# A decoder layer in fp32: keys and values made a batch ahead and kept in HBM, and the experts' second product in seven half-size products

## The chip, the cores and the metric

The kernel runs on one core of one Trainium2 chip. The metric is the time of the program on the device in microseconds (us); lower is better. The program was run three times: median 5657.23 us, from 5656.19 to 5658.22. One further execution was profiled; all rows of the profile come from it.

## What is computed

The reference is a decoder layer on x of 8 batches x 512 tokens x 512 features, in fp32. Three blocks follow one another, each with a residual and a layernorm: a selective state-space block (inner width 1024, 16 states, scanned along the tokens), a cross-attention to a context of the same shape, and a feed-forward block with 32 routed experts and a shared one. Cut to what the change touches:

```python
# cross-attention, 16 heads of 32; ctx is key and value input
qm = _split_heads(q @ Wq.T + bq)
km = _split_heads(ctx @ Wk.T + bk)
vm = _split_heads(ctx @ Wv.T + bv)
scores = einsum('bnlh,bnph->bnlp', qm, km) / sqrt(32)       # masked
out = einsum('bnlp,bnph->bnlh', softmax(scores), vm)        # then @ Wo.T + bo

# experts: each of 32 takes at most cap = 640 tokens, 4 experts per token
xe = xp[buf_tok].reshape(E, cap, DIM)
h = silu(einsum('ecd,edh->ech', xe, w1)) * einsum('ecd,edh->ech', xe, w3)
out = einsum('ech,ehd->ecd', h, w2) * buf_w.reshape(E, cap, 1)
y = zeros((N + 1, DIM)).at[buf_tok].add(out.reshape(E * cap, DIM))[:N]
z = silu(xf @ sw1) * (xf @ sw3) @ sw2                       # shared expert
```

The values depend on the context alone, and so do the keys: neither needs the output of the state-space block.

## The kernel before, in words

`program` (L1272) runs three stages: `layers`, `experts`, `finish`.

**`layers` (L82)** goes through 16 chunks of 256 tokens, two per batch (L949). A chunk has 32 steps (L950), and each step scans 4 states of 128 channels on VectorE: a product (L446), the scan (L450) and a product with C (L467), for which ScalarE makes the decays (L434) and TensorE sums over the states (L471, into `py`; `gated` L483 takes it up). The C and B values come by DMA broadcast (`bcast`, L378), and the step sizes by a copy across partitions (L423). Between the steps stand the chunk's own products: `back` of the chunk before (L500), `gate_x` and `convolve` of this and the next (L302).

Cross-attention, router and shared expert of a batch are a list of small units, built by `units(b)` (L649). The list of batch b - 1 is worked off during the two chunks of batch b: `side` (L997), each unit with a weight that stands for its time on TensorE, handed out in step with the chunk's own weights (L1050 to L1055). So batch 0 has no such list beside it, and the list of the last batch runs after all chunks, alone (L1072). A list begins with the load of Wv, of the context (`cT`) and of the mask, then four `values` units and four `keys` units, each 4 matmuls of 128x512 (`dense`, L679, L682) and one copy out of PSUM (L690, L702); then four `flip` units that load x1 (the output of the state-space block, `fetch` L668) and transpose it, then `queries`. `spread` (L716) lays two heads' keys and queries into operand tiles by DMA, two pairs of heads ahead. `maximum`, `weigh` and `gather` (L735, L761, L777) are the attention, `output`, `flip2`, `hidden` and `shared` the rest; `send` (L638) scatters the tokens to the experts' buffer in HBM, `xbuf`. Values lie in `va`, a single tile; keys in `kT`. The tiles s1 to s4 are four large buffers that the list's stages pass on to one another; weights rotate through the two `wa` buffers. Some order within a queue is the compiler's: the trace shows several DMAs and sums earlier than the program's text has them (the context of the next batch is issued at 826.9 us, its first use is at 944.3).

**`experts` (L1077)**: for each expert `load` (L1101) fetches its 640 rows and three weights. `flip` (L1136) transposes the rows, `sums_x` and `sums_w` (L1144, L1127) form sums and differences of the blocks, and `hidden` (L1157) computes both hidden products with seven block products for eight (L1152, 320 columns). `give` (L1213) multiplies one tile of 128 tokens with w2 (L1218, four matmuls of 512 columns), scales the rows (L1222) and adds them into `based` by an indirect DMA on GpSimd (L1223); it runs five times per expert, between the transposes of the next. Each source matmul is two instructions in the trace. **`finish` (L1257)** reloads `based`, normalizes and stores.

Of the kernel before, what the change touches and what calls it, by code (L numbers as in the profile page):

```python
# [16 lines left out]
P = 128  # L17
B, S, D = 8, 512, 512
DC = D // P
# [14 lines left out]
HD = 32  # L34
SC = S // P

E = 32
# [42 lines left out]


def layers(ctx, tc, a, x1d, filld, based, xbuf):  # L82

# [44 lines left out]
    def rows(w):  # L128
        return w.rearrange("(c p) f -> p c f", p=P)
# [95 lines left out]
    def quad(tag, name):  # L225
        return big(tag, name)[:, 0 : DC * S].rearrange("p (c t) -> p c t", c=DC)
# [407 lines left out]
    def send(j, st):  # L634

        for k in range(K):
# [12 lines left out]
    def units(b):  # L649

        st = {}
        todo = []

        def unit(weight):
            return lambda fn: todo.append((weight, fn, False))

        @unit(0)
        def _():
# [11 lines left out]
        def flip(j):  # L670
# [4 lines left out]
            for dc in range(DC):  # L675
                nc.tensor.transpose(ps[:, dc, :], xr[:, dc * P : (dc + 1) * P], ident)
            return lambda: nc.scalar.copy(st["x1T"][:, :, j * P : (j + 1) * P], ps) and None

        def dense(lhs, rhs):  # L679
            ps = psm.tile([P, S], F32, tag="mm", name="ps_p")  # L680
            for dc in range(DC):
                nc.tensor.matmul(ps, lhs(dc), rhs(dc), start=(dc == 0), stop=(dc == DC - 1))  # L682
            return ps

        def values(pc):
            if pc == 0:
                load("Wk")
            w, cT = loaded["Wv"], st["cT"]
            ps = dense(lambda dc: cT[:, dc, pc * P : (pc + 1) * P], lambda dc: w[:, dc, :])
            return lambda: nc.scalar.copy(  # L690
                va[:, pc].rearrange("p i (j d) -> p i j d", d=HD)[:, :, 0:3:2, :],
                ps.rearrange("p (i j d) -> p i j d", j=2, d=HD),
            ) and None

        def keys(oc):
            if oc == 0:
                load("Wq")
                st["kT"] = quad("s4", "kT")
            w, cT = loaded["Wk"], st["cT"]
            ps = dense(lambda dc: w[:, dc, oc * P : (oc + 1) * P], lambda dc: cT[:, dc, :])  # L700

            return lambda: nc.vector.scalar_tensor_tensor(  # L702
                st["kT"][:, oc, :], ps, bk[:, oc : oc + 1], st["mk"], ALU.add, ALU.mult
            ) and None

        def queries(oc):
            if oc == 0:
# [124 lines left out]
        def flip2(j):  # L832
            if j == 0:
                load("sw3")
                st["x2T"] = quad("s4", "x2T")
            ps = psm.tile([P, DC, P], F32, tag="mm", name="ps_tr")
            for dc in range(DC):
                nc.tensor.transpose(ps[:, dc, :], st["x2"][j][:, dc * P : (dc + 1) * P], ident)
            return lambda: nc.scalar.copy(st["x2T"][:, :, j * P : (j + 1) * P], ps) and None

        def hidden(name, ic):
            x2T = st["x2T"]
            if name == "sw1" and ic == 0:
                st["hT"] = quad("s3", "hT")
# [12 lines left out]

            return use
# [25 lines left out]
        for j in range(DC):  # L884
# [192 lines left out]
def experts(ctx, tc, a, xbuf, based):  # L1077
# [32 lines left out]
    def A(w, i, j):  # L1110
        return w[:, 2 * j : 2 * j + 2, i * FH : (i + 1) * FH]

    def B(x, j, k):
        return x[:, 2 * j : 2 * j + 2, k * HALF : (k + 1) * HALF]

    def sums_w(got, n):

        w = got[n]
        s1, s2, s4 = (wp.tile([P, 2, FH], F32, tag=f"{n}s{i}", name="s") for i in (1, 2, 4))
# [19 lines left out]
    def sums_x(got):  # L1139

        x = got["xT"]
        t1, t2, t4 = (p2.tile([P, 2, HALF], F32, tag=f"t{i}", name="t") for i in (1, 2, 4))
        got["t"] = t1, t2, B(x, 0, 1), t4
        nc.vector.tensor_tensor(t1, B(x, 0, 1), B(x, 0, 0), ALU.subtract)  # L1144
        nc.vector.tensor_tensor(t2, B(x, 1, 1), t1, ALU.subtract)
        nc.vector.tensor_tensor(B(x, 0, 1), B(x, 1, 1), B(x, 0, 1), ALU.subtract)
        nc.vector.tensor_tensor(t4, B(x, 1, 0), t2, ALU.subtract)

    def product(ps, w, r, x, more=False):

# [59 lines left out]
            product(xs[m], A(w, 1, 1), r, t4, more=True)  # L1210
            use(m, 1, 0, xs[m])

    def give(e, got, j):  # L1213

        xe = got["x"]
        po = pso.tile([P, D], F32, tag="po", name="po")
        for ic in range(DC):
            nc.tensor.matmul(  # L1218
                po, got["hT"][:, ic, j * P : (j + 1) * P], got["w2"][:, ic, :], start=(ic == 0), stop=(ic == DC - 1)
            )  # L1220
        y = p2.tile([P, D], F32, tag="y", name="y", bufs=CJ + 1)
        nc.scalar.activation(y, po, AF.Identity, scale=xe[:, j, D + e : D + e + 1])  # L1222
        nc.gpsimd.indirect_dma_start(  # L1223
            out=based,
            out_offset=bass.IndirectOffsetOnAxis(ap=xe.bitcast(I32)[:, j, D + E :], axis=0),
            in_=y,
            in_offset=None,
            bounds_check=N + P - 1,
            compute_op=ALU.add,
        )  # L1230

    nxt = load(0)
    for j in range(CJ):
# [4 lines left out]
            pass  # L1238
    for e in range(E):
        got, nxt = nxt, load(e + 1) if e + 1 < E else None  # L1240
        got["hT"] = p2.tile([P, DC, CAP], F32, tag="hT", name="hT")
        for r in range(2):
            hidden(got, r, sums_w(nxt, "w1") if nxt and r else iter(()))
        side = sums_w(nxt, "w3") if nxt else iter(())

        for n, j in enumerate(reversed(range(CJ))):
            if nxt:
                flip(nxt, n)
                if n == CJ - 1:
                    sums_x(nxt)  # L1250
            next(side, None)
            give(e, got, j)
        for _ in side:
            pass


def finish(ctx, tc, based, out):  # L1257
# [61 lines left out]
```

## Time and profile before

| what | us |
|---|---|
| median of three runs (range) | 5657.23 (5656.19 to 5658.22) |
| the profiled execution | 5660.41 |
| its span, first to last instruction | 5658.7 |
| TensorE busy / VectorE / ScalarE / GpSimd | 4933.6 / 4107.3 / 2548.5 / 525.2 |
| values and keys of batch 0: first instruction | 472.1 |
| last batch's list alone, from its first product to its last | 3745.4 to 3976.8 |
| first transposes of the experts | 3996.0 |
| start to start of two experts' w2 products | 49.51 |
| reload of `based` issued | 5601.2 |

How to read the profile: a row of the groups names a line, an engine, an operation, what it writes and reads, how often it occurs, then busy time, the mean duration of one, and the engine's idle time before them with what ended it. PE is TensorE's matmul, PEld its weight load, DVE VectorE, ACT ScalarE, POOL GpSimd, SPq the queue of DMAs that SyncE issues. The timeline has start, duration, engine, line and operation in order of time, and in brackets how long the engine was idle before and what released it. The clock of TensorE is given as granted share of its full rate.

### The profile page before, as it was taken

How to read it: one execution, taken by the hardware profiler on the slowest of the kernel's cores; microseconds unless marked ns; L12 is line 12 of the kernel's file. 1: busy time of each engine (PE TensorE's matmuls, PEld its weight loads, DVE VectorE, ACT ScalarE, POOL GpSimd, SP SyncE). 2: the span in 40 equal slices, each digit the busy share in tenths (PEclk: the TensorE clock that was granted, in tenths of full speed). 3: DMA queues.
4: the chain of work that ended last, by engine and by line, in shares of the span. 5: the costliest groups of instructions: out<-in, count | busy, mean ns of one | idle time of the engine just before them, and what ended most of it. 6: DMA issues, size and time to landing. Idle time of an engine off the chain costs nothing. (4 is left out here: it accounts for less than half of the span.)

```text
span 5658.7 us, 57578 instructions
## 1 busy us (share of the span) xinstructions
PE 4933.6 (87%) x18984; PEld 2576.2 (46%) x18984; DVE 4107.3 (73%) x5290; ACT 2548.5 (45%) x5347; POOL 525.2 (9%) x424
## 2 busy tenths in 40 slices
PE   5658889888988988988898898889899999999994
PEld 3334344334434433434443443333566666666662
DVE  5998988989899898898999999834444444444443
ACT  4454565654655456565465646513122222222223
POOL 0000001002000200200200020010211111111111
PEclk8778999999999999999999999999999999999997
DMA  7675345335433634544443363331544444444444
GB/s 205 192 225 176 96 127 164 110 116 158 137 105 108 188 95 127 162 112 117 159 136 105 110 194 94 107 110 43 159 123 115 118 125 115 119 117 123 115 118 137
DMA packets 484635, 744.49 MB, mean 132 GB/s; under 512 B 68170, under 2 KB 200810, under 8 KB 484336
## 3 DMA queue, kind: packets, MB, share of 16 engines
q1 hardware_dynamic: 446832, 655.52, 38.1%
q0 software_dynamic: 33280, 76.90, 7.1%
q10 hardware_dynamic: 4224, 8.39, 0.4%
q8 instruction: 150, 2.46, 0.2%
q14 instruction: 149, 1.22, 0.1%
HBM read 491.91 MB, written 148.28 MB: 113 GB/s over the span
## 5 line engine op out<-in xcount | busy, mean ns | idle before, releaser
L434 ACT ACTIVATE l_da<-both,l_aneg 128x256 f32<-128x256 f32 x2048 | 894.0, 499 | 837.6 <-DVE h L450 795.6
L450 DVE TENSOR_TENSOR_SCAN h<-l_da,h 128x1028 f32<-128x1028 f32 x512 | 1172.4, 2295 | 55.0 <-ACT h L440 28.7
L471 PE MATMUL py<-h,l_twice 128*64 128x256 f32 x4096 | 632.4, 421 | 225.9 <-DVE h L467 225.7
L446 DVE TENSOR_TENSOR h<-both,bc 128x1024 f32<-128x1024 f32 x512 | 619.5, 1217 | 125.2 <-PE py L471 58.3
L467 DVE TENSOR_TENSOR h<-h,bc 128x1024 f32<-128x1024 f32 x512 | 624.1, 1221 | 6.3 <-DVE l_state L452 0.3
L1218 PE MATMUL po<-w,hT 128*128 128x512 f32 x1280 | 575.1, 592 | 0.0
L471 PEld LDWEIGHTS py<-h,l_twice 128*64 128x64 f32 x4096 | 297.9, 147 | 588.1 <-DVE h L467 262.0
L735 PE MATMUL ps_s<-l_ka,l_qa 64*128 64x512 f32 x1024 | 316.9, 698 | 140.8 <-DVE mx L737 140.6
L1152 PE MATMUL ps_h<-xT,w 128*128 128x320 f32 x1536 | 436.7, 434 | 0.0
L1173 DVE TENSOR_TENSOR hT<-ps_h,p 128x320 f32<-128x320 f32 x128 | 63.0, 492 | 443.4 <-PE ps_h L1152 443.4
L1223 POOL DMA_INDIRECT based<-y,xe x160 | 252.2, 1576 | 1358.8 <-ACT y L1222 828.6
L737 DVE TENSOR_REDUCE mx<-ps_s 128x2 f32<-128x1024 f32 x256 | 310.9, 1217 | 81.6 <-PE ps_s L735 81.0
L1222 ACT ACTIVATE y<-po,xe 128x512 f32<-128x512 f32 x160 | 110.0, 688 | 551.7 <-PE po L1218 542.6
L1152 PEld LDWEIGHTS ps_h<-xT,w 128*128 128x128 f32 x1536 | 292.9, 191 | 131.8 <-issue 15.8
L1218 PEld LDWEIGHTS po<-w,hT 128*128 128x128 f32 x1280 | 231.1, 190 | 231.6 <-issue 224.1
L761 PE MATMUL ps_t<-l_qa,l_ka 64*128 64x512 f32 x1024 | 303.3, 655 | 12.9 <-ACT eT L765 9.0
L765 ACT ACTIVATE eT<-ps_t 128x1024 f32<-128x1024 f32 x256 | 258.9, 1013 | 108.3 <-PE ps_t L761 108.0
L777 PE MATMUL po<-eT,l_va 128*64 128x512 f32 x1024 | 278.8, 623 | 21.2 <-ACT raw L789 18.1
L1152 PE MATMUL ps_h<-t,s 128*128 128x320 f32 x1024 | 286.2, 432 | 0.0
L682 PE MATMUL ps_p<-x2T,wa 128*128 128x512 f32 x512 | 249.6, 639 | 21.1 <-DVE hT L852 19.2
L500 PE MATMUL po<-wm,zs 128*128 128x512 f32 x512 | 241.6, 623 | 21.5 <-DMA wm<-in_out_proj_w 21.5
L302 PE MATMUL ps_z<-xnT,wm 128*128 128x256 f32 x1024 | 241.6, 389 | 12.7 <-DMA wm<-in_in_proj_w 12.7
(205 smaller groups left out, 6695.3 us busy)
## 6 DMA issues: line engine op xcount, KB each, us to landing
bc<-scr SPq DMA_DIRECT2D x1024, 128.0 KB
w<-in_w SPq DMA_DIRECT2D x96, 1024.0 KB
wm<-in_in_proj_w SPq DMA_DIRECT2D x128, 512.0 KB
xbuf<-zero SPq DMA_DIRECT2D x32, 1362.5 KB
xe<-xbuf SPq DMA_DIRECT2D x32, 1362.5 KB
both<-dt SPq DMA_DIRECT2D x256, 128.0 KB
both<-dtx SPq DMA_DIRECT2D x256, 128.0 KB
wm<-in_out_proj_w SPq DMA_DIRECT2D x64, 512.0 KB
```

The lines of the kernel that those rows point to most:

```text
L434: nc.scalar.activation(da[:, n, 1:], dt[:, c % 2, j, :], AF.Exp, scale=aneg[:, c, j, g, m : m + 1])
L446: nc.vector.tensor_tensor(steps, dtx[:, c % 2].unsqueeze(2).to_broadcast([P, 2, NG // 2, T]), bc[0], ALU.mult)
L450: nc.vector.tensor_tensor_scan(flat, da.rearrange("p n t -> p (n t)"), flat, 0.0, ALU.mult, ALU.add)
L467: nc.vector.tensor_tensor(steps, steps, bc[1], ALU.mult)
L471: nc.tensor.matmul(py[j * HP : (j + 1) * HP, c % 2, :], twice, h[:, j * 2 + m, 1:], start=False, stop=(s == (NST // NG - 1, NG // 2 - 1, 1)),)
L735: nc.tensor.matmul(ps[:, j, :], qa[r, lt * P : (lt + 1) * P], ka[r, :], start=True, stop=True)
L737: return lambda: nc.vector.tensor_reduce(mx[:, lt, :].unsqueeze(2), ps, AX.X, ALU.max) and None
L761: nc.tensor.matmul(ps[:, j, :], ka[r, kc * P : (kc + 1) * P], qa[r, :], start=True, stop=True)
L765: nc.scalar.activation(eT, ps, AF.Exp)
L777: nc.tensor.matmul(po[j * 2 * HD : (j + 1) * 2 * HD, :], va[:, kc, i, j * HD : (j + 2) * HD], eT[:, j, :], start=(kc == 0), stop=(kc == SC ...
L1152: nc.tensor.matmul(ps, w[:, n, r * P : (r + 1) * P], x[:, n, :], start=not more and n == 0, stop=n == 1, skip_group_check=more,)
L1218: nc.tensor.matmul(po, got["hT"][:, ic, j * P : (j + 1) * P], got["w2"][:, ic, :], start=(ic == 0), stop=(ic == DC - 1))
```

## The change

There are two independent parts.

**Keys and values.** The units `values` and `keys` leave `units(b)` and go to a new list, `sources(b)`. Their results are written to two HBM tiles (512x512 each, two buffers) instead of `va` and `kT`. `sources(b + 1)` is worked off with `units(b)`, and `sources(0)` during batch 0, which had no list. `units(b)` begins with eight DMAs that bring the values from HBM into `va` (runs of 32 numbers), and `spread` takes the keys from HBM. The buffer s4 is gone: `x2T` moves to s3 and the shared expert's `hT` to s2, which the context also uses.

**Experts.** `give` now handles all five tiles of an expert. The first four (512 tokens) and the two halves of w2's rows and columns form a 2x2 block product done in seven products for eight, each of two 128-row tiles, two 128-deep parts and 256 columns; the fifth tile stays four matmuls of 512 columns. The sums of the hidden values (`sums_w(got, "hT")`) are made at its start, those of w2 (`sums_w2`) during the first half of `hidden`. The indirect adds come in the order tile 4, 0, 1, 2, 3. `hT` and its sums have one buffer.

```diff
+    def sources(b):
+        st, todo = {}, []
+        def begin():
             load("Wv")
             st["cT"] = cT = quad("s2", "cT")
             nc.sync.dma_start(cT, rows(a["ctx"][b]))
...
+            kept[b] = [dp.tile([S, D], F32, tag="vd", name="vd"), dp.tile([D, S], F32, tag="kd", name="kd")]
+        def values(pc):
...
+            def put():
+                v = p3.tile([P, D], F32, tag="row", name="v")
+                nc.scalar.copy(v, ps)
+                nc.sync.dma_start(kept[b][0][pc * P : (pc + 1) * P, :], v)
...
+        def keys(oc):
...
+            def put():
+                k = p3.tile([P, D], F32, tag="row", name="k")
+                nc.vector.scalar_tensor_tensor(k, ps, bk[:, oc : oc + 1], st["mk"], ALU.add, ALU.mult)
+                nc.sync.dma_start(kept[b][1][oc * P : (oc + 1) * P, :], k)
...
     def units(b):
+        def begin():
+            if b == B - 1:
+                load("Wq")
             st["x1T"] = quad("s1", "x1T")
+            vd, st["kd"] = kept.pop(b)
+            for pc in range(SC):
+                for j in range(2):
+                    nc.sync.dma_start(
+                        va[:, pc, :, 2 * j * HD : (2 * j + 1) * HD],
+                        vd[pc * P : (pc + 1) * P, :].rearrange("p (i j d) -> p i j d", j=2, d=HD)[:, :, j, :],
+                    )
...
-                nc.sync.dma_start(ka[r1 : r1 + HD, :], st["kT"][r0 : r0 + HD, i // 2, :])
+                h0 = (2 * i + j) * HD
+                nc.sync.dma_start(ka[r1 : r1 + HD, :], st["kd"][h0 : h0 + HD, :])
...
-        for j in range(SC):
-            add(3.4, values, j)
-        for j in range(DC):
-            add(3.4, keys, j)
-            if j == 2:
-                add(0, fetch, 0)
+        more = sources(b + 1) if b + 1 < B else []
+        todo += more[:-2]
+        add(0, begin)
+        add(0, fetch, 0)
+        todo += more[-2:]
...
-        if t == 0 and b:
-            side, spent = units(b - 1), 0.0
+        if t == 0:
+            side, spent = units(b - 1) if b else sources(0), 0.0
...
+    def sums_w2(got):
+        w = got["w2"]
+        got["t2"] = t1, t2, t3, t4 = [wp.tile([P, 2, FH], F32, tag=f"w2t{i}", name="t", bufs=1) for i in range(4)]
+        for o, x, y in (
+            (t1, BW(w, 0, 1), BW(w, 0, 0)),
+            (t2, BW(w, 1, 1), t1),
+            (t3, BW(w, 1, 1), BW(w, 0, 1)),
+            (t4, BW(w, 1, 0), t2),
+        ):
+            nc.vector.tensor_tensor(o, x, y, ALU.subtract)
+            yield
...
+    def give(e, got, side):
...
+        for _ in sums_w(got, "hT"):
+            pass
+        s1, s2, s3, s4 = got["hT", "s"]
+        next(side, None)
+        for r in both:
+            xs.append(psx.tile([P, HALF], F32, tag="h", name="ps_o")[:, 0:FH])
+            product(xs[r], A(hT, 0, 0), r, BW(w2, 0, 0))
+            p1.append(keep(xs[r], r, "p1", r))
...
+        nc.scalar.activation(ys[j], po, AF.Identity, scale=weight(j))
+        put(j)
+        next(side, None)
+        for r in both:
+            ps = psy.tile([P, HALF], F32, tag="h2", name="ps_o")[:, 0:FH]
+            product(ps, A(hT, 0, 1), r, BW(w2, 1, 0))
+            use(r, 0, ps, p1[r])
+        for r in both:
+            product(xs[r], s2, r, t2, more=True)
+            pu.append(keep(xs[r], r, "pu", r))
+        next(side, None)
+        zs = []
+        for r in both:
+            zs.append(psy.tile([P, HALF], F32, tag="h2", name="ps_o")[:, 0:FH])
+            product(zs[r], s1, r, t1)
+            p5.append(keep(zs[r], r, "p5", 2 + r))
+        for r in both:
+            product(xs[r], s3, r, t3, more=True)
+            use(2 + r, 1, xs[r], p5[r])
+        next(side, None)
+        for r in both:
+            product(zs[r], s4, r, BW(w2, 1, 1), more=True)
+            use(r, 1, zs[r], pu[r])
+            put(r)
+        next(side, None)
+        for r in both:
+            product(xs[r], A(hT, 1, 1), r, t4, more=True)
+            nc.scalar.activation(ys[2 + r][:, 0:FH], xs[r], AF.Identity, scale=weight(2 + r))
+            put(2 + r)
...
     for e in range(E):
...
-            hidden(got, r, sums_w(nxt, "w1") if nxt and r else iter(()))
+            hidden(got, r, sums_w2(got) if r == 0 else sums_w(nxt, "w1") if nxt else iter(()))
+        give(e, got, between(nxt) if nxt else iter(()))
```

`keep` scales a partial sum by the row's weight on ScalarE into SBUF, `use` adds it to another on VectorE, `put` is the indirect add, and `between` yields the transposes and sums of the next expert one at a time, where `next(side, None)` stands.

More of the change, by code (lines that the diff above doesn't have):

```diff
@@ L647, in send @@
             tc.add_to_no_dep_group("slots", put.ins)
[L649 to L658, printed above, removed]
+    kept = {}
+    def sources(b):
+        st, todo = {}, []
+        def begin():
             load("Wv")
@@ L663, in _, with dense, units @@
             nc.sync.dma_start(mk, a["mask"][b : b + 1, :].to_broadcast([P, S]))
-            st["x1T"] = quad("s1", "x1T")
+            kept[b] = [dp.tile([S, D], F32, tag="vd", name="vd"), dp.tile([D, S], F32, tag="kd", name="kd")]
+        def values(pc):
+            if pc == 0:
+                load("Wk")
+            w, cT = loaded["Wv"], st["cT"]
+            ps = dense(lambda dc: cT[:, dc, pc * P : (pc + 1) * P], lambda dc: w[:, dc, :])
+            def put():
+                v = p3.tile([P, D], F32, tag="row", name="v")
+                nc.scalar.copy(v, ps)
+                nc.sync.dma_start(kept[b][0][pc * P : (pc + 1) * P, :], v)
+            return put
+        def keys(oc):
+            if oc == 0 and b:
+                load("Wq")
+            w, cT = loaded["Wk"], st["cT"]
+            ps = dense(lambda dc: w[:, dc, oc * P : (oc + 1) * P], lambda dc: cT[:, dc, :])
+            def put():
+                k = p3.tile([P, D], F32, tag="row", name="k")
+                nc.vector.scalar_tensor_tensor(k, ps, bk[:, oc : oc + 1], st["mk"], ALU.add, ALU.mult)
+                nc.sync.dma_start(kept[b][1][oc * P : (oc + 1) * P, :], k)
+            return put
+        todo.append((0, begin, False))
+        for j in range(SC):
+            todo.append((3.4, lambda j=j: values(j), False))
+        for j in range(DC):
+            todo.append((3.4, lambda j=j: keys(j), False))
+        return todo
+    def dense(lhs, rhs):
+        ps = psm.tile([P, S], F32, tag="mm", name="ps_p")
+        for dc in range(DC):
+            nc.tensor.matmul(ps, lhs(dc), rhs(dc), start=(dc == 0), stop=(dc == DC - 1))
+        return ps
+    def units(b):
+        st = {}
+        todo = []
+        def begin():
+            if b == B - 1:
+                load("Wq")
+            st["x1T"] = quad("s1", "x1T")
+            vd, st["kd"] = kept.pop(b)
[5 more added lines that the diff above has]
+                    )
         def fetch(j):
@@ L677, in flip @@
             return lambda: nc.scalar.copy(st["x1T"][:, :, j * P : (j + 1) * P], ps) and None
[L679 to L704, printed above, removed]
         def queries(oc):
@@ L834, in flip2 @@
                 load("sw3")
-                st["x2T"] = quad("s4", "x2T")
+                st["x2T"] = quad("s3", "x2T")
             ps = psm.tile([P, DC, P], F32, tag="mm", name="ps_tr")
@@ L843, in hidden @@
             if name == "sw1" and ic == 0:
-                st["hT"] = quad("s3", "hT")
+                st["hT"] = quad("s2", "hT")
             if name == "sw3" and ic == 0:
@@ L1111, in A, with BW @@
         return w[:, 2 * j : 2 * j + 2, i * FH : (i + 1) * FH]
+    def BW(w, j, k):
+        return w[:, 2 * j : 2 * j + 2, k * FH : (k + 1) * FH]
     def B(x, j, k):
@@ L1118, in sums_w @@
         w = got[n]
-        s1, s2, s4 = (wp.tile([P, 2, FH], F32, tag=f"{n}s{i}", name="s") for i in (1, 2, 4))
+        s1, s2, s4 = (wp.tile([P, 2, FH], F32, tag=f"{n}s{i}", name="s", bufs=1 if n == "hT" else 2) for i in (1, 2, 4))
         got[n, "s"] = s1, s2, A(w, 1, 0), s4
@@ L1211, in hidden, with weight, keep, use @@
             use(m, 1, 0, xs[m])
-    def give(e, got, j):
-        xe = got["x"]
+    def give(e, got, side):
+        xe, hT, w2 = got["x"], got["hT"], got["w2"]
+        t1, t2, t3, t4 = got["t2"]
+        both = range(2)
+        ys = [p2.tile([P, D], F32, tag="y", name="y", bufs=CJ + 2) for j in range(CJ)]
+        def weight(j):
+            return xe[:, j, D + e : D + e + 1]
+        def keep(ps, r, tag, j):
+            v = p2.tile([P, HALF], F32, tag=f"{tag}{r}", name=tag)[:, 0:FH]
+            nc.scalar.activation(v, ps, AF.Identity, scale=weight(j))
+            return v
+        def use(j, k, ps, more):
+            nc.vector.scalar_tensor_tensor(ys[j][:, k * FH : (k + 1) * FH], ps, weight(j), more, ALU.mult, ALU.add)
+        def put(j):
+            nc.gpsimd.indirect_dma_start(
+                out=based,
+                out_offset=bass.IndirectOffsetOnAxis(ap=xe.bitcast(I32)[:, j, D + E :], axis=0),
+                in_=ys[j],
+                in_offset=None,
+                bounds_check=N + P - 1,
+                compute_op=ALU.add,
+            )
+        for _ in sums_w(got, "hT"):
+            pass
+        s1, s2, s3, s4 = got["hT", "s"]
+        next(side, None)
+        xs, p1, pu, p5 = [], [], [], []
+        for r in both:
+            xs.append(psx.tile([P, HALF], F32, tag="h", name="ps_o")[:, 0:FH])
+            product(xs[r], A(hT, 0, 0), r, BW(w2, 0, 0))
+            p1.append(keep(xs[r], r, "p1", r))
+        j = CJ - 1
@@ L1216, in give @@
         po = pso.tile([P, D], F32, tag="po", name="po")
         for ic in range(DC):
[L1218 to L1230, printed above, removed]
+            nc.tensor.matmul(po, hT[:, ic, j * P : (j + 1) * P], w2[:, ic, :], start=(ic == 0), stop=(ic == DC - 1))
@@ L1232, in experts, with between @@
+    def between(nxt):
+        sums = sums_w(nxt, "w3")
+        for j in range(CJ):
+            flip(nxt, j)
+            if j == CJ - 1:
+                sums_x(nxt)
+            next(sums, None)
+            yield
     nxt = load(0)
@@ L1240, in experts @@
         got, nxt = nxt, load(e + 1) if e + 1 < E else None
-        got["hT"] = p2.tile([P, DC, CAP], F32, tag="hT", name="hT")
+        got["hT"] = p2.tile([P, DC, CAP], F32, tag="hT", name="hT", bufs=1)
         for r in range(2):
-            hidden(got, r, sums_w(nxt, "w1") if nxt and r else iter(()))
[L1244 to L1254, printed above, removed]
+            hidden(got, r, sums_w2(got) if r == 0 else sums_w(nxt, "w1") if nxt else iter(()))
+        give(e, got, between(nxt) if nxt else iter(()))
 def finish(ctx, tc, based, out):
```

## The prediction

> **What bounds the kernel now.** First the digits of the span in 40 slices, for the stages: the columns are 141 us each.
>
> ```profile
> PE   5658889888988988988898898889899999999994
> DVE  5998988989899898898999999834444444444443
> ```
>
> Three regimes. Up to slice 26 VectorE is at nine tenths, TensorE a little under it; then a piece with TensorE alone; from slice 28 (the experts) TensorE is full and VectorE at four tenths. The busy time by stage (columns: stretch, its length, busy us of PE, PEld, DVE, ACT, POOL, then granted clock, DMA share, GB/s) puts numbers on them: the first batch, the second, the eighth, the last batch's attention that runs alone, the experts.
>
> ```profile
> 40.00:440.00 400.00, 240.21 (x1032) 135.87 (x1030) 358.60 (x376) 216.81 (x505) 18.41 (x20) 0.75 0.71 215
> 440.00:905.00 465.00, 404.66 (x1642) 193.77 (x1643) 419.59 (x489) 266.60 (x562) 10.37 (x13) 0.93 0.43 124
> 3230.00:3695.00 465.00, 404.91 (x1634) 184.68 (x1634) 421.38 (x475) 251.71 (x543) 29.85 (x20) 0.94 0.43 127
> 3695.00:3990.00 295.00, 252.13 (x808) 100.61 (x808) 103.88 (x199) 67.88 (x90) 32.00 (x35) 0.92 0.26 85
> 4040.00:5530.00 1490.00, 1490.00 (x5176) 927.26 (x5175) 630.85 (x1112) 368.33 (x752) 238.33 (x151) 1.00 0.46 118
> ```
>
> The experts have not one idle microsecond on TensorE in 1490 us: what is taken off it there comes off the time. The first batch has 160 us of TensorE free; the lone piece is TensorE's too, with holes. Those holes are in its timeline (start, us, engine, line, count, [idle before <- what ended it]):
>
> ```profile
> 3735.81 9.80 PE L500 MATMUL po<-wm,zs 128*128 128x512 f32 x16 [4.92 <-DMA wm<-in_out_proj_w]
> 3745.44 13.90 PE L682 MATMUL ps_p<-wa,cT 128*128 128x512 f32 x32
> 3759.18 13.90 PE L682 MATMUL ps_p<-cT,wa 128*128 128x512 f32 x32
> ...
> 3779.39 1.94 PE L676 MATMUL ps_tr<-l_ident,xr 128*128 128x128 f32 x8 [4.82 <-DMA xr<-x1d]
> 3782.01 15.76 PE L682 MATMUL ps_p<-x1T,wa 128*128 128x512 f32 x32 [0.68 <-ACT x1T L677]
> ```
>
> The two rows of cT are the values and keys of the last batch: 3745.4 to 3772.9, 27.5 us. A source matmul shows as two instructions. Last, a pass of 256 columns, and the end of the experts:
>
> ```profile
> 466.46 3.62 PE L302 MATMUL ps_z<-xnT,wm 128*128 128x256 f32 x16
> ```
> ```profile
> 5570.36 17.33 PE L1218 MATMUL po<-w,hT 128*128 128x512 f32 x40
> 5574.96 1.54 POOL L1223 DMA_INDIRECT based<-y,xe  x1 [25.47 <-ACT y L1222]
> ...
> 5596.10 1.54 POOL L1223 DMA_INDIRECT based<-y,xe  x1 [3.77 <-DMA based<-y,xe]
> 5601.17 27.91 SPq L1266 DMA_DIRECT2D acc<-based  x8
> ```
>
> **The products with w2.** A stream's last instruction shows its mean duration (592 ns for 512 columns, 389 for 256: the groups), so the pace is (17.33 - 0.59)/39 = 0.429 us for 512 columns and (3.62 - 0.39)/15 = 0.215 us for 256. Before: five token tiles x 4 matmuls x 2 passes x 0.429 = 17.2 us an expert. After: the first four tiles take 7 products x 2 x 2 = 28 matmuls of 256 columns, 56 x 0.215 = 12.05; the fifth stays, 8 x 0.429 = 3.43; together 15.5. The gain is 1.68 us (a tenth, not an eighth, since a fifth of the tokens is outside). The start-to-start time of the experts is 49.51 us, so it falls to 47.8.
>
> A rule speaks against halving the width. The group of weight loads for these passes has 190 ns each, at either width. The Trainium skill, "TensorE: Matmul & The Clock Gate", Part 3, says that a weight load overlaps a running matmul only where the row group differs, and here all 128 rows are used (its Part 2 allows a second way, a background buffer). By that rule a pass costs 190 + 215 ns, the 56 + 8 passes 27.6 us against 40 x 619 ns = 24.8, and the change loses 2.9 us an expert, 91 us in all. By the row above it is 215 ns with the load inside, at full clock and with another load for each pass. I take the row; only 25 ns of it are spare.
>
> New work beside it, per expert: VectorE gets eight sums of 128x512 (0.685 us each, the group of L1127) and six evictions of 128x256 from PSUM (below the 0.49 us of L1173's 128x320): at most 8.4 us on 21.0 (42% of 49.5). ScalarE loses five y at 0.69 and gets one at 0.69 and eight of at most 0.43, +0.7 us on 12. Both lie beside TensorE. What they must meet: the hidden product ends, the last multiply (0.49) and the sums s1, s2 (1.4) end about 2.2 us later, while TensorE first has a transpose, the first two products and the fifth tile, 5.6 us, and uses s2 only after 9; the single transpose buffer comes round every 1.7 us at the least and its copy is 0.69. The w2 sums stand among the evictions of the first half of the hidden stage: each delays an eviction by 0.69, where two PSUM buffers leave some 3 us. If that cover fails, TensorE waits 0.7 us at up to four places. I take 0.
>
> The scatter-adds change place: five at one a tile before; now the fifth tile's early and four in a burst at the end. Each waits for the one before, 5.3 us. For the last expert this is the path: before, first at +4.6 and the reload at +30.8 us after L1218 starts. Now the first is at +6.3 and the second needs row tile 0 complete, 15.5 - 2.6 + 0.9 = +13.8, then 4 x 5.3: +35.0. So 4 us are given back. Experts: 31 x 1.68 - 4 = **-48 us**, with ends -30 (0.6 us of waits an expert) and -52.
>
> **Values and keys one batch ahead.** The same eight units per batch, shifted: the first batch gets eight, the lone piece loses eight; batches in between trade.
>
> Lone piece: 27.5 us go, but the queries behind them need x1 of the chunk just finished. Its projection ends at 3745.6, its layernorm issues the write at 3750.6. The two transposes of 3779.39 show issue (3773.6) to use at 5.8 us for such a load, just behind a 1 MB weight load. I take 3 us for the write and 4 for the read, then 2 us of transposes and copies: queries at 3759.5 instead of 3782.0. **-23 us**; -18 if both transfers take 5.8, -27.5 if the wait vanished. So the next late thing here is x1's round trip. Wq and the values' reload replace Wv, Wk and ctx in the queue; gather first reads them some 50 us later.
>
> First batch: TensorE +27.5 us into 160 free, VectorE +4 x 0.74 (L702) = 3. What TensorE costs VectorE is in the waits of VectorE for py in all batches (us in total, times, longest):
>
> ```profile
> DVE h L446 <- PE py L471: 58.3, 25, 7.8
> DVE zs L483 <- PE py L471: 38.6, 19, 4.3
> DVE h L446 <- DMA bc<-scr: 17.6, 8, 9.0
> ```
>
> Of the 97 us of py, 9 are in the first batch; the other 88 are 12.6 a batch for 165 us more TensorE, 0.076 each: 27.5 x 0.076 = 2. And 5 MB more through queues at 0.71: I take 3. **+8 us**, from +3 (VectorE alone) to +25 (each unit holds VectorE for all its 3.4 us).
>
> Batches 1 to 7: same products, new transfers. Values and keys out, 2 MB in 2 KB packets: 1024 x 84 ns / 16 = 5.4 us of the engines (packet records). Values back: 8 DMAs of 1,024 runs of 128 bytes. "DMA: Bandwidth & Descriptors", Specifications, wants 512 bytes for line rate and below it a read-modify-write; the records have 11 ns for 128 bytes, so 8192 x 11 / 16 = 5.6 us, twice that if the rule bites (estimate); the sixteen loads of l_aneg, as many packets, were issued within 10.9 us, so 5.6 to 11. On 200 us busy (0.43 x 465) that is 8%, of VectorE's DMA waits (bc, both, xt: 60 us in eight batches) 0.6 us a batch. SyncE's queue gets 16 issues of 0.58; the eight writes wait for the copy out of PSUM, and the broadcasts for the scan stand behind them. They run about two steps (14 us) ahead. I take 1 us a batch, **+7 us**; 0 to +21. Keys from HBM instead of SBUF are fetched two pairs ahead: 0. ctx now shares a buffer with the shared expert's hidden values, but from the end of `shared` to the first values lie 32 us (912.5 to 944.3): 0; uncovered it would be some 7 us.
>
> **Sum.** -48 - 23 + 8 + 7 = -56 on a span of 5658.7: 5602.7. The profiled run has 5660.4 around that span, 3.2 above the runs' median 5657.2, so 5601 to compare with the median. About 0.2% (11 us) is what a measurement of this kernel can tell from no change.
>
> **Rivals.**
> - The layers take it for nothing (slack already there, x1's trip short): 5601 - 15 - 4 = 5582. For it: 160 us free. Against: VectorE at 90% and DMA at 0.71 there. 0.17.
> - The experts get a new wait. Their xe buffer is freed by the last scatter-add:
>
> ```profile
> 4607.03 1.54 POOL L1223 DMA_INDIRECT based<-y,xe  x1 [4.06 <-ACT pu L1166]
> 4612.14 0.37 SPq L1104 DMA_DIRECT2D xe<-xbuf  x1
> ```
>
>   That is +32 us after the products start at 4580.6; in the burst it becomes +37, and the next transposes are at +47.8. The first xe took 7.1 us, so 4 us are left. A scatter-add at 6.5 us instead of 5.4 uses them up. 1 us late each: 5632. 0.13.
> - x1's trip replaces the moved products: the lone piece gains 10 only: 5614. 0.07.
> - Slower: the broadcasts queue behind the writes and the 128-byte reload, and the scan stalls. It has 71 us to eat, in eight batches: from 9 us a batch there is no gain; at 12 it is 5682. Against: bc cost 17.6 us in all, 9 of them once, though such writes (L797, L751) stand in the queue already. 0.04.
> - Likeliest: 5601. 0.59.
>
> Cases within 11 us of before come from the second and fourth rival's middle: 0.03; slower 0.03; faster 0.94. The range, 5578 to 5636, takes in the first three rivals and the unknown costs of each part.
>
> **What would show it.** Experts: start-to-start 47.8 with TensorE still 100% busy; 56 + 8 passes at 215 and 429 ns. If xe is named before the transposes, the second rival. Lone piece: queries near 3759 minus the drift, the wait named x1d or xr. First batch: near 408. Middle batches: 465 each within 2; bc waits above 40 us would show the fourth. Wrong if passes of 256 take 400 ns, or if a middle batch grows by 5 us.

## The result, and the profile after

The changed kernel takes 5615.94 us (median of four runs, 5606.99 to 5620.4) against 5657.73 beside it: a ratio of 0.9917, 95% interval 0.9902 to 0.9933. It is faster by 0.8%, 15 us above the forecast of 5601 and inside its range. Run once more on another chip it took 5615.04, ratio 0.9919 [0.9905, 0.9932]. The profiled execution took 5620.06 us, its span is 5617.3.

The busy time by stage, in the stretches of the prediction (columns as there: stretch, length, busy us of PE, PEld, DVE, ACT, POOL, clock, DMA share, GB/s):

```profile
40.00:440.00 400.00, 265.74 (x1085) 144.90 (x1083) 354.74 (x375) 216.53 (x502) 21.44 (x20) 0.79 0.72 219
440.00:905.00 465.00, 396.37 (x1608) 188.87 (x1608) 410.77 (x462) 264.39 (x554) 11.66 (x13) 0.91 0.47 134
3230.00:3695.00 465.00, 405.21 (x1631) 186.94 (x1630) 419.18 (x472) 255.78 (x545) 33.11 (x21) 0.94 0.46 134
3695.00:3990.00 295.00, 245.01 (x817) 96.80 (x815) 121.38 (x231) 76.17 (x106) 31.99 (x35) 0.91 0.25 82
4040.00:5480.00 1440.00, 1439.04 (x5888) 1062.63 (x5887) 854.24 (x1534) 399.64 (x872) 235.05 (x150) 1.00 0.48 122
```

The experts are still TensorE alone: 1439.04 of 1440 us. VectorE went from 42% to 59% there, weight loads from 62% to 74%, and neither shows on TensorE. In the first batch TensorE is busier by 25 us and VectorE gets less done in the same 400 us (354.74 for 358.60): something else holds it. In the second batch TensorE and VectorE both do about 8 us less in the same 465.

The lone piece, timeline of the changed kernel (start, us, engine, line, count, [idle before <- what ended it]):

```profile
3758.25 9.69 PE L503 MATMUL po<-wm,zs 128*128 128x512 f32 x16 [8.52 <-DMA wm<-in_out_proj_w]
...
3772.97 0.37 SPq L515 DMA_DIRECT2D x1d<-o  x1
3775.80 4.99 SPq L725 DMA_DIRECT2D xr<-x1d  x4
...
3778.50 1.94 PE L733 MATMUL ps_tr<-l_ident,xr 128*128 128x128 f32 x8 [9.06 <-DMA xr<-x1d]
3781.11 17.07 PE L703 MATMUL ps_p<-x1T,wa 128*128 128x512 f32 x32 [0.68 <-ACT x1T L734]
```

The two rows of cT are gone, and the wait that takes their place is x1's round trip: 2.8 us from the write's issue to the read's, 2.7 to the first use. From the end of the last projection (3767.9) to the queries it is 13.2 us, where it was 36.4.

The experts' passes, and the rows of the next expert (timeline):

```profile
4552.48 1.54 POOL L1279 DMA_INDIRECT based<-y,xe  x1 [4.12 <-ACT p L1213]
4557.14 0.37 SPq L1135 DMA_DIRECT2D xe<-xbuf  x1
...
4565.70 0.60 PE L1170 MATMUL ps_t<-e_ident,xe 128*128 128x128 f32 x4
...
4571.73 1.89 PE L1199 MATMUL ps_o<-w,hT 128*128 128x256 f32 x8
4573.46 1.89 PE L1199 MATMUL ps_o<-t,s 128*128 128x256 f32 x8
```

Eight passes of 256 columns start 1.73 us apart, 216 ns each. From expert to expert it is 47.86 us in 26 of the 31 steps. The load of xe is issued 8.6 us ahead of the transposes (before, some 17.6), and no wait stands before these. The end (timeline):

```profile
5530.86 1.54 POOL L1279 DMA_INDIRECT based<-y,xe  x1 [19.91 <-ACT y L1302]
...
5538.43 1.54 POOL L1279 DMA_INDIRECT based<-y,xe  x1 [6.03 <-DVE y L1276]
...
5543.95 1.54 POOL L1279 DMA_INDIRECT based<-y,xe  x1 [3.98 <-DMA based<-y,xe]
5549.29 1.54 POOL L1279 DMA_INDIRECT based<-y,xe  x1 [3.80 <-DMA based<-y,xe]
5554.70 1.54 POOL L1279 DMA_INDIRECT based<-y,xe  x1 [3.87 <-DMA based<-y,xe]
5559.51 2.93 SPq L1366 DMA_DIRECT2D acc<-based  x4
```

The four late adds follow one another at 5.4 us. The first waits for its rows (`y`), each of the other three for the add before it. The last product ends at 5540.2, so the reload comes 19.3 us later instead of 13.5.

All traces of the study were cut at the same instructions. The table has, in us, how much longer (+) each stretch is than in the kernel before: the first batch (first gate product of chunk 0 to that of chunk 2); the first chunk of batch 1; the remaining chunks to the end of the last projection; from there to the last batch's queries; on to the first expert's transposes; to the last product; to the reload of `based`.

| kernel | batch 0 | chunk (1,0) | rest | lone piece | to experts | experts | to reload |
|---|---|---|---|---|---|---|---|
| changed | +11.3 | +7.2 | +4.4 | -23.2 | +5.3 | -51.9 | +5.8 |
| changed, second run | +11.2 | +4.4 | +3.9 | -23.1 | +5.0 | -52.9 | +5.6 |
| only the products with w2 | +1.8 | -0.5 | -5.5 | +0.1 | +2.3 | -52.9 | +5.8 |
| only keys and values ahead | +10.1 | +8.2 | +5.2 | -23.0 | +5.3 | -1.3 | +0.4 |
| last batch's alone ahead | +9.0 | -2.9 | +0.5 | -23.0 | +7.8 | -53.2 | +6.1 |
| the same, second run | +9.4 | +0.7 | +7.2 | -23.1 | +5.2 | -52.8 | +6.0 |
| values in long runs | +10.0 | +6.4 | -0.1 | -23.1 | +4.7 | -52.2 | +6.1 |
| a quarter of the first sources | +11.8 | +4.4 | +9.8 | -23.1 | +2.0 | -52.9 | +6.1 |
| DMAs by GpSimd | +7.9 | +1.1 | -0.1 | -23.0 | +2.8 | -52.0 | +5.7 |
| the same, second run | +9.3 | -0.1 | -8.4 | -23.2 | +3.1 | -52.3 | +5.0 |
| writes alone by GpSimd | +7.9 | +1.0 | -13.3 | -23.1 | +3.5 | -51.2 | +6.3 |
| last batch's, end as before | +9.8 | +1.7 | -5.3 | -23.3 | +4.8 | -50.7 | +0.4 |
| GpSimd, end as before | +8.6 | +1.1 | -9.2 | -23.1 | +4.9 | -49.2 | 0.0 |

Two traces of one kernel, taken on different chips, differ by up to 8 us in the long stretch "rest", by under 4 in chunk (1,0), by up to 2.6 on the way to the experts, by a few tenths in the lone piece and about 1 in the experts. So the third column is read only with several traces.

### The profile page after: what moved, and what is told of

It is laid out like the page before. It is cut to its first block, busy times and chain, and to the rows that moved or that the text cites. A ratio compares the mean times of both kernels' runs of the same rounds, so it can differ in the third digit from the quotient of the medians.

```text
span 5617.3 us, 60406 instructions
## 1 busy us (share of the span) xinstructions
PE 4888.6 (87%) x19752; PEld 2725.6 (49%) x19752; DVE 4351.5 (77%) x5738; ACT 2592.2 (46%) x5480; POOL 546.1 (10%) x424
## 5 line engine op out<-in xcount | busy, mean ns | idle before, releaser
L641 POOL DMA_INDIRECT xbuf<-x2t,dest x128 | 216.7, 1693 | 622.1 <-DVE dest L635 583.7
L305 PE MATMUL ps_x<-xnT,wm 128*128 128x256 f32 x1024 | 245.3, 393 | 1.4 <-ACT xnT L294 1.1
L305 PEld LDWEIGHTS ps_z<-xnT,wm 128*128 128x128 f32 x1024 | 196.2, 196 | 83.7 <-ACT l_da L437 27.1
```

The source lines that it names most:

```text
L305: nc.tensor.matmul(ps[:, i, :], w[:, dc, i * P : (i + 1) * P], f["xnT"][:, dc, :], start=(dc == 0), stop=(dc == DC - 1),)
```

## The experiments

**Each part alone.** The layers of before with the experts of after, and the reverse.

> The experts' seven half-size products alone; keys and values as before. Theory 1 (the two parts add up, and nearly the whole gain is the experts'): -52 us on TensorE from the first transposes to its last product, +6 us of scatter-adds at the end, so about -46 us, near 5611. Theory 2 (both parts gain, each about half, and something in the layers eats one of them together with the other): -25 us or less.

> Keys and values one batch ahead alone; the experts as before. Theory 1 (the piece alone gains 23 us, but the layers before it take 22 of them back): within 5 us of before, 5653 to 5662. Theory 2 (the layers' loss belongs to the meeting with the experts' change or is scatter): -15 to -25 us, 5633 to 5643. Projection of the last chunk near 3768 by theory 1, near 3750 by theory 2.

The products alone: 5614.24, ratio 0.9922 [0.9909, 0.9935]. Keys and values alone: 5661.51, ratio 1.0004 [0.9995, 1.0012]. The parts add up (0.9926 against 0.9917), and the whole gain is the experts'. Keys and values ahead gain the 23 us at the lone piece (row four of the table) and pay as much elsewhere.

**Only the last batch's keys and values ahead.** They are made in batch 0 and kept in HBM; the other batches make theirs as before, with the buffer s4 (`early` chooses in `units`).

```diff
-            side, spent = units(b - 1) if b else sources(0), 0.0
+            side, spent = units(b - 1) if b else sources(B - 1), 0.0
+        early = b == B - 1
```

> The experts as after; of the keys and values only those of batch 7 are made early, during batch 0, and kept in HBM; batches 0 to 6 make theirs as before, without HBM. If the loss in the layers comes from batch 0 alone: the same +11 there, nothing later, projection of the last chunk near 3757, total near 5605. If it comes from the transfers and the shifted lists of batches 1 to 7 as well: those 11 us come back as said, so 11 us faster than after. If neither (drift of any new schedule): as slow as after, 5616.

It took 5601.0, ratio 0.9894 [0.988, 0.9908]; later 5605.0, 0.9907 [0.9892, 0.9922]. The lone piece gains the same 23 us, batch 0 still pays 9, and the extra time of chunk (1,0) is gone in both runs. What is paid there therefore belongs to what the change does in every batch. This run takes out three things at once: the traffic through HBM, the shifted list and the buffer that the context shares. Its intervals overlap those of the changed kernel, so it is the stretches that tell.

**Values in long runs.** They are kept in HBM in the layout of `va`, with its ones, so that a row tile comes back in one DMA of 3 KB runs instead of two of 128 bytes (1.5 MB of values a batch each way, not 1).

```diff
-            kept[b] = [dp.tile([S, D], F32, tag="vd", name="vd"), ...]
+            kept[b] = [dp.tile([S, 3 * D // 2], F32, tag="vd", name="vd"), ...]
-                for j in range(2):
-                    nc.sync.dma_start(va[:, pc, :, 2 * j * HD : (2 * j + 1) * HD], ...)
+                nc.sync.dma_start(va[:, pc].rearrange("p i f -> p (i f)"), vd[pc * P : (pc + 1) * P, :])
```

> As after, but the values lie in HBM in the layout of their tile, ones included, so that they come back in four DMAs with runs of 3 KB in place of eight with runs of 128 bytes (1.5 MB for 1). If the 128-byte runs cost the layers anything: the last chunk's projection 3 to 10 us earlier than in after and the waits on DMA shorter. If they cost nothing: within 3 us of after.

5613.48, ratio 0.9924 [0.9911, 0.9937]: no difference from the changed kernel that can be told. Chunk (1,0) keeps its +6.4. The short runs are not the cause.

**A quarter of the first products.** In batch 0 one matmul in place of four for each value and key unit: the sums cover 128 of the 512 features.

```diff
-            ps = dense(lambda dc: cT[...], lambda dc: w[:, dc, :])
+            ps = dense(lambda dc: cT[...], lambda dc: w[:, dc, :], DC if b else 1)
```

> The changed kernel with one matmul in place of four in each of the eight products of batch 0's keys and values (batch 0's keys and values are partial sums over 128 of 512 features); loads, copies out of PSUM, writes to HBM and their order in the program stay. The first batch of the changed kernel is 11.3 us longer than before. If TensorE's time is the cause (the sums over the states, py, come later), three quarters of the 27.5 us go and the first batch is longer by 3 to 5 only: 5609. If the transfers are the cause (5 MB more through busy queues, or issues in SyncE's queue), it stays near 11: 5616.

5619.31, ratio 0.9935 [0.9922, 0.9949], and batch 0 stays at +11.8. Three quarters of TensorE's 27.5 us there are gone, and nothing comes back. VectorE's waits in batch 0, between the cuts of the table (us in total, times, longest): before,

```profile
DVE zs L483 <- PE py L471: 8.9, 5, 2.7
DVE st L73 <- DMA xt<-in_x: 4.6, 1, 4.6
DVE o L509 <- PE po L500: 3.2, 1, 3.2
```

and after,

```profile
DVE zs L486 <- PE py L474: 9.8, 5, 3.2
DVE st L73 <- DMA xt<-in_x: 9.5, 1, 9.5
DVE o L512 <- PE po L503: 3.8, 1, 3.8
PE po L503 <- DVE k L688: 4.5, 2, 4.0
```

The sums `py` are late by 0.9 us more. The load of x is late by 4.9, and a new row has the projection wait for VectorE's copy of keys out of a PSUM buffer that both use. All of VectorE's waits between the cuts come to 37.0 us before and 42.8 after, its work to 369.3 and 372.9: 9.3 of the 11.3 us. The load of x is not the root: with the writes issued by GpSimd (below) its row is all but gone, another of 8.2 us stands there, and batch 0 is still 7.9 longer.

```profile
DVE zs L486 <- ACT zs L356: 8.2, 1, 8.2
DVE st L73 <- DMA xt<-in_x: 0.5, 1, 0.5
```

In SyncE's queue (timelines), before and then after:

```profile
227.03 0.58 SPq L487 DMA_DIRECT2D o<-in_x  x1
227.70 0.93 SPq L262 DMA_DIRECT2D wm<-in_out_proj_w  x2
...
294.37 0.60 SPq L271 DMA_DIRECT2D xt<-in_x  x1
```
```profile
242.79 0.53 SPq L675 DMA_DIRECT2D vd<-v  x1
247.37 0.33 SPq L689 DMA_DIRECT2D kd<-k  x1
...
252.38 0.60 SPq L490 DMA_DIRECT2D o<-in_x  x1
253.08 0.93 SPq L265 DMA_DIRECT2D wm<-in_out_proj_w  x2
...
300.20 0.60 SPq L274 DMA_DIRECT2D xt<-in_x  x1
```

The projection's weights are fetched 25 us later, and the next chunk's x 6 us later. That the writes stand ahead of them is not the reason: in the next version, which takes them out of this queue, the weights leave at 253.2 as well.

**The sixteen DMAs of a batch issued by GpSimd** instead of SyncE: the same bytes, another queue.

```diff
-                nc.sync.dma_start(kept[b][0][pc * P : (pc + 1) * P, :], v)
+                nc.gpsimd.dma_start(kept[b][0][pc * P : (pc + 1) * P, :], v)
-                nc.sync.dma_start(kept[b][1][oc * P : (oc + 1) * P, :], k)
+                nc.gpsimd.dma_start(kept[b][1][oc * P : (oc + 1) * P, :], k)
...
-                    nc.sync.dma_start(
+                    nc.gpsimd.dma_start(
                         va[:, pc, :, 2 * j * HD : (2 * j + 1) * HD],
```

> The changed kernel with the eight writes and the eight reloads of a batch issued by GpSimd instead of SyncE. If batches 1 to 7 lose their 11.6 us because these DMAs stand in SyncE's queue ahead of the loads of x and of weights, these come back: 5604. If the loss is TensorE's or the transfers' own (the same bytes, the same engines), it stays: 5616. If GpSimd's issues are dearer than SyncE's or wait for the copies out of PSUM in front of the work of the convolution, 5620 to 5640.

5600.97, ratio 0.9897 [0.9882, 0.9912]. Because this was measured beside other kernels than the changed one, the two were then measured on one chip, together with a version that moves the writes alone.

> The changed kernel itself, beside the next three on one chip: 5616 within 5. By the theory of the queue its extra 7 us in the first chunk of batch 1 come again; if they were chance, they do not.

> The version with the sixteen DMAs of a batch issued by GpSimd, on this chip: if SyncE's queue is the cause, 5601 within 5 and some 15 below the changed kernel; if the first run's 5601 was this chip's scatter, no difference from the changed kernel.

> Only the eight writes of values and keys to HBM are issued by GpSimd; the eight reloads of the values stay with SyncE. If the writes are what hurts (each waits at the head of SyncE's queue for a copy out of PSUM, with loads of weights behind it), about 5602, as with both moved. If the eight reloads in a row hurt, 5614.

The changed kernel 5615.04; all sixteen by GpSimd 5596.94, ratio to before 0.989 [0.9876, 0.9904]; the eight writes alone 5596.23, 0.9888 [0.9874, 0.9902]. The writes are the whole of it: issued by SyncE they cost 18.8 us (5615.04 - 5596.23), the reloads of the values nothing that can be told. Among VectorE's waits in batches 1 to 7 (us in total, times, longest, from 470 to 3760 us) these follow the writes: before, after, and with the writes moved,

```profile
DVE h L446 <- PE py L471: 58.3, 25, 7.8
DVE xs L336 <- ACT xs L328: 22.2, 16, 3.1
```
```profile
DVE h L449 <- PE py L474: 45.4, 27, 3.7
DVE xs L339 <- ACT xs L331: 33.0, 21, 4.7
...
DVE k L688 <- DMA vd<-v: 2.5, 4, 1.1
```
```profile
DVE h L449 <- PE py L474: 28.9, 27, 3.7
...
DVE xs L339 <- ACT xs L331: 20.1, 15, 1.5
```

`py` are the sums over the states, 16.5 us less with the writes out of the queue; `xs` is the convolution's taps, 12.9 less. The second traces (the changed kernel, and all sixteen moved) have 42.9 and 34.9 for `py`, 31.5 and 23.3 for `xs`. The row of k is direct: a copy of keys waits until a write of values has left the `row` buffer, and has no counterpart with the writes moved.

Neither of the two large rows ends with a DMA. In these stretches TensorE has no idle time over 0.3 us before a product that the taps need (`ps_x`), in any of these traces. Where it does wait for weights, for the gate's products, moving the writes gives nothing back (after, then moved):

```profile
PE ps_z L305 <- DMA wm<-in_in_proj_w: 28.4, 12, 5.8
```
```profile
PE ps_z L305 <- DMA wm<-in_in_proj_w: 29.6, 10, 6.7
```

For the projection's weights it waits 8.5 and 5.2 us. So late weights do not account for the cost. SyncE's queue itself stands at the writes for 44 us in these batches (42 in the second trace), mostly in these rows of the changed kernel:

```profile
SPq L689 <- DVE k L688: 25.1, 15, 3.5
...
SPq L675 <- ACT v L674: 9.9, 10, 1.9
```

Two waits of VectorE that came with the change stay, whichever queue writes: for the load of x (8.9 before, 26.9 after, 22.5 with the writes moved) and for ScalarE's part of `dtx` (5.2, 27.0, 27.1). With the last batch's alone ahead they are 8.7 and 6.2.

What this doesn't separate: a write that waits at the head of the queue, and the order that the compiler then gives to everything else. With another queue the order of the products on TensorE changes too. It is shown that the writes cost by standing in SyncE's queue; which of the two ways is open.

**The end, and the experts' start.** On top of the version with the last batch's keys and values alone, the last expert keeps its full-width products (`give_rows`, the `give` of before), and w1's first load is to follow xe.

```diff
+        if nxt:
+            give(e, got, between(nxt))
+        else:
+            for j in reversed(range(CJ)):
+                give_rows(e, got, j)
```

> The version with only the last batch's keys and values moved (5601.0), with two more changes: the last expert's products with w2 stay whole, in eight, so that its five indirect adds go out one by one as before, and the load of the first expert's w1 is held behind that of its rows. If the 5.8 us between the last product and the reload of based come from the burst of indirect adds, that stretch goes back from +5.8 to about 0 against before, while the last expert's products take 1.7 us more: -4. If the wait at the experts' start comes from w1's load going ahead of xe, the start comes about 2.5 us earlier. Together 5595 by this theory. If the end is set by something else (the reload's own wait for all stores), or w1 then comes late in place of xe, 5601 or a little more.

> The same kernel as the one with only the last batch's keys and values moved, on this chip beside the next version: 5601 within 5.

5601.4, ratio 0.9903 [0.9888, 0.9919], against 5605.01, 0.9907 [0.9892, 0.9922], beside it: the totals do not tell them apart. The stretch to the reload is back from +6.0 to +0.4, as expected, and the experts' products longer by 2.1. The other half came to nothing: in the trace w1's load still leaves ahead of xe (3973.62 and 3974.24), so the wait at the experts' start, 21.3 us, was not put to the test. Last, both gains together: all sixteen DMAs by GpSimd, and the end as before.

> All sixteen DMAs issued by GpSimd, and the last expert's products with w2 whole, so that its indirect adds go out one by one. If the two gains add up: 5601 - 5.3 for the reload of based + 1.3 for the longer products = 5597. If the end is already covered, 5601.

5594.2, ratio 0.988 [0.9864, 0.9895]: the fastest version, and its interval overlaps that of the writes moved alone (0.9888). Its end (timeline):

```profile
5503.75 17.33 PE L1347 MATMUL po<-w,hT 128*128 128x512 f32 x40
...
5529.82 1.54 POOL L1352 DMA_INDIRECT based<-y,xe  x1 [3.70 <-DMA based<-y,xe]
5534.58 2.84 SPq L1389 DMA_DIRECT2D acc<-based  x4
```

The reload is 30.8 us after the products' start, as it was in the kernel before. In the changed kernel the burst makes it 35.0 (5559.51 - 5524.53).

## Why the prediction was right, and where it was not

**Experts, -48: measured -46.1** (-51.9 and +5.8; the second run -47.3). Mechanism and size hold: 1.65 us an expert for 1.68, and the late adds behind one another. The reload was put at 35.0 us after the last products' start, and is there; before it was at 30.8. So 31 x 1.65 - 4.2 = 47.0; four longer steps in this trace take about 2 us more (two in the second trace, 1). The Trainium skill's rule weighed against it, "TensorE: Matmul & The Clock Gate", Part 3 (a weight load overlaps a running matmul only where the row group differs), would have made an expert 52.4 us by the prediction's estimate; with all 128 rows used it is 47.86. The row decided rightly. The end of before spoke against the rule already: by the estimate its 40 passes would be 24.8 us, 619 ns each, and they took 17.33.

**Lone piece, -23: measured -23.2.** The round trip was put at 3 and 4 us, and is 2.8 and 2.7. But the sum stopped at the queries. Behind them 5.3 us are lost again (5.0 in the second run), of which the products alone lose 2.3 too. The idle time before the first transposes is 21.6 us for 19.1; in the trace w1's load is issued ahead of xe, 3990.40 and 3991.05, where before xe came first. And the 32 matmuls of the queries take 17.07 us for 15.76. Both times they start at half the clock, here for 6.2 us and before for 3.6, and 2.6 us at half speed are the 1.3 lost. The granted clock is the third number from the end; the same microsecond, after and before:

```profile
3786.00:3787.00 1.00, 1.00 (x2) 0.34 (x1) 0.00 (x0) 0.00 (x0) 0.00 (x0) 0.50 0.00 0
```
```profile
3786.00:3787.00 1.00, 1.00 (x4) 0.51 (x3) 0.00 (x0) 0.00 (x0) 0.00 (x0) 1.00 0.00 0
```

The other 1.5 us were not traced. Net the piece is worth 18, the end that the prediction gave it if both transfers took 5.8: a right bound for a wrong reason.

**First batch, +8: measured +11.3.** The total is near, its terms are not. All of it lies in the first chunk (+12.3, then -0.9). TensorE's products were put at 2 us and cost nothing (a quarter of them left: +11.8). VectorE's 3 are 3.0, four copies of 0.75. "5 MB more through queues, I take 3" is the term that was too small: about 8 us are left for it. At most 3.4 of them are the writes' place in the queue, for with these moved +7.9 to +9.3 stay. The trace shows the weights of the projection and x late in SyncE's queue, and a projection that waits for the keys' copy; which of the loads, of the order and of the shared PSUM buffer does it was not separated.

**Batches 1 to 7, +7: measured +11.6 and +8.3.** The size is near, the shape is wrong: "1 us a batch" does not exist. By the same cuts batch 1 is 5.0 us longer (2.1 in the second run), batches 2 to 5 together are 1.1 shorter (4.3), and batches 6 and 7 are 7.7 longer (10.4). A middle batch 5 us longer was one of the prediction's own signs of being wrong, and it came: batch 1 in the first trace, batch 6 with 6.4 in the second. The prediction saw the writes wait for the copy out of PSUM, with others behind them, then took the broadcasts for the victims. Their waits fell instead, from 8.6 to 2.3 us (4.9) in these batches; what the writes cost stands before the sums over the states and the convolution's taps. With the writes moved this stretch is 12.3 us shorter than before (1.0 - 13.3, in the fastest of that version's five executions), 8.5 with all sixteen in one trace and 1.0 longer in the other; a gain the prediction didn't have, and uncertain in size.

**The two parts.** For keys and values the terms make -23 + 8 + 7 = -8. Alone they measured 1.0004 of before, no gain that can be told. So the total came out because the experts' term is large and good; for the other part the prediction's sign was not confirmed.

The 15 us that are missing: 5.3 behind the queries, 4.6 in batches 1 to 7, 3.3 in batch 0, 1.9 in the experts, about half of it their 0.03 us each.

**The rule on short runs.** The Trainium skill, "DMA: Bandwidth & Descriptors", Specifications, asks for 512 bytes; the prediction took 5.6 us of the engines a batch, or 11 by the rule. With runs of 3 KB the kernel takes 5613.48 for 5615.94, within the scatter. So it is hidden. The trace speaks for the first price: the 8192 packets of 128 bytes of the first reload took 13.0 ns each, 6.7 us of the engines.

**The rivals.** The layers did not take it for nothing (5582), though with the writes on another queue and the old end the kernel comes to 5594. xe was no new wait, but it was nearer than reckoned: its load was put at 37 us after the products' start and left at 38.9 (4557.14 for the product at 4518.27), 8.6 us before its use. With the prediction's 7.1 us for the load that leaves 1.5, not 4. x1's trip did not replace the moved products. The slower case had the place right, SyncE's queue, and the victim wrong; the price was a quarter of the 71 us that it needed, 18.8.

## What to carry to other kernels

Half-size products paid here because TensorE is full without a hole and a pass, 216 ns, is still longer than its weight load: the gain is read off the pass times and arrives nearly whole, except where a burst at the end is the path. When work moves, follow the DMAs that it issues: eight writes a batch, each waiting for a copy, cost 18.8 us more in SyncE's queue than in GpSimd's. And moving only what was exposed, one batch in eight, got the same 23 us without the traffic of the other seven. Last, a sum that stops where a wait ends misses what the shift does behind it, here 5.3 us of the 23.

## What the hardware showed beside this

- A pass of 256 columns takes 216 ns with another 128x128 weight load of some 180 ns (1062.63 us of PEld over 5887) inside each: the loads are 74% busy over 1440 us and leave no gap.
- Indirect adds to one tensor follow at 5.4 us, each released by the one before, once their data are there. One of five sent early leaves a chain of four: the reload comes at 35.0 us after the products' start, and at 30.8 where the five go out one by one.
- TensorE's clock after a gap: with 2.97 us of work in the 13 us ahead of the queries, they ran at 0.50 for their first 6.2 us and at 1.00 from there; with 7.10 us of work in the 13 us ahead, for 3.6 us.
- Issued by GpSimd, a write holds it for 0.54 us in the median; GpSimd's busy time rises from 546 to 574 us in the whole kernel, and no row of waits names these writes.
